# Weighted sum of values in an attention stage: values stationary on four column groups of 32, exponentials streamed

## The chip, the cores and the metric

The kernel runs on one core of a Trainium2 chip. The metric is the device time of one execution in microseconds. The profile shows one execution instruction by instruction, on five engines: PE (TensorE, with its weight loads shown apart as PEld), DVE (VectorE), ACT (ScalarE), POOL (GpSimd) and SP (SyncE, which issues DMAs here).

## What is computed

Two layers on an image of 48 channels and 256 x 256 pixels. Layer 0 normalises by groups, makes queries, keys and values by a pointwise product and a 3 x 3 depthwise convolution, cuts them into 4 x 4 patches and runs an attention of 8 heads over the patches. Layer 1 normalises again and multiplies windows of 64 x 64 along width, height and channels. The part that the change touches is the attention:

```python
        qkv = jnp.einsum('bchw,oc->bohw', x, w_qkv)
        qkv = dwconv3x3(qkv, w_dw)
        q, k, v = jnp.split(qkv, 3, axis=1)
        def heads(t):
            u = unfold(t)
            return u.reshape(b, NUM_HEADS, u.shape[1] // NUM_HEADS, u.shape[2])
        q, k, v = (heads(q), heads(k), heads(v))
        q = _l2norm(q)
        k = _l2norm(k)
        attn = jnp.einsum('bhcn,bhcm->bhnm', q, k) * temperature
        attn = jax.nn.softmax(attn, axis=-1)
        out = jnp.einsum('bhcn,bhnm->bhcm', v, attn)
```

A head has 96 channels. Inside the image there are 4,096 patches, which the kernel treats as n (queries) and m (keys); patches of the border are zeros and enter as a constant in the denominators. The softmax runs over m for each n, and the output is a sum over n: for each head, out[c, m] = sum over n of v[c, n] / z[n] * e[n, m], where e are exponentials of logits and z their sums.

## The kernel before

**Heads and iterations.** The attention stage is a loop over 8 heads (`h`), and in each over 16 iterations (`g`) of two blocks of 128 queries. The order of instructions on every engine in this loop is the order in which the program is written (`manual_schedule`)[...].

In one iteration:
- `normalised` (L585 to L591, VectorE, four short instructions) adds the sums of a block's exponentials, takes the reciprocal and scales the block's values into `vn`, 128 queries by 96 channels.
- `scores` (L337 on TensorE and L572 on ScalarE) makes the logits of one block against all 4,096 keys, in four pieces of 1,024, and their exponentials `e`. It is called for the second block of this iteration and then for the first block of the next, so that ScalarE's work lies under TensorE's.
- `weigh` (L601) makes the weighted sums of the iteration's two blocks, in four parts `k` of 8 key blocks. The stationary operand is 64 columns of `e` (64 keys), the streamed operand is `vn` (96 columns): the result has keys on the partitions, 64 at a time, in two column groups of the array. Each part is 32 matmuls; the trace shows each of them, being fp32, as two instructions. Each part fills one tile of the pool `big` (three tiles of two PSUM banks, which the logits and the strips use too).
- VectorE adds each part to an accumulator in SBUF (`oacc`, L612, 128 x 768; L610, a copy, in a head's first iteration).

**Stores.** The result has keys on the partitions, but memory wants channels there. In a head's last iteration, `store` transposes the accumulators on TensorE (L618, four transposes for 512 keys, into a tile of the pool `one`), copies them with ScalarE (L621) and stores them with two DMAs issued by GpSimd (L623). Parts of the last iteration's sums are stored while the next part is computed; the last two pieces of 512 keys follow in the next head's iteration 0, after its logits, or after the loop for the last head.

**The pool `one`** has two PSUM banks, given out in turn. In it lie `pn` (L247, the norms of a row of depthwise work, read by VectorE at L251), `pst` (L555, the next head's values turned by TensorE, copied by ScalarE at L557; two tiles in each of g = 11 to 14, and one in each of g = 1 to 6 of head 0) and `pt` (above).

**Work of the next head in the same loop.** Heads 0 to 6 carry the depthwise convolution of the following head, ten rows of patches, one row started in each iteration from g = 0 on. In iteration g, VectorE does the norm (about twelve short instructions, L251 to L268) and the scale (L274) of row g-2, and eight taps (L228) of row g-1: three after the scale, five after the second `normalised`. All this comes in VectorE's queue ahead of the iteration's adds. ScalarE squares row g-1 (L239) after the taps; VectorE sums the squares (L243) after the first add. TensorE's `pn` of row g-1 comes at the start of the next iteration. Head 0 also has strips (L177 and L180), TensorE and ScalarE work that the second and fourth parts of `weigh` are followed by.

Of the kernel before, what the change touches and what calls it, by code (L numbers as in the profile page):

```python
# [8 lines left out]
F32 = mybir.dt.float32  # L9
# [13 lines left out]
NH = 8  # L23
HD = C * KK // NH
# [15 lines left out]
TP = 256  # L40
# [5 lines left out]
def conv_preact_kernel(  # L46
# [15 lines left out]
    nc = tc.nc  # L62
# [15 lines left out]
    os_ = dram.tile([NT // TP, C * KK, TP], F32, name="os_")  # L78
# [3 lines left out]
    ident = const.tile([128, 128], F32, name="ident")  # L82
# [15 lines left out]
    for s in range(2):  # L98
        r = slice(s * C, (s + 1) * C)
        for h in range(NH if s == 0 else H0):  # L100
            o = s * M0 + h * HC if h < H0 else (h - H0) * HC
            nc.gpsimd.dma_start(
                out=(wq[r] if h < H0 else wr[0:C])[:, o : o + HC].rearrange("c (z e) -> c z e", z=3),
                in_=w_qkvT.rearrange("c (z h e) -> h c z e", z=3, h=NH)[h],
# [4 lines left out]
    for z in range(3):  # L109
        for j in range(CH):  # L110
            p = (z * CH + j) * 6
# [50 lines left out]
    class Strip:  # L162
# [24 lines left out]
        def store(self):  # L187
            for s, rows in enumerate(both_halves(t1[1], 2 * self.j, 2, base=1)):
                nc.sync.dma_start(out=rows, in_=self.ot[:, 2 * s : 2 * s + 2, :])
# [111 lines left out]
    NB = NT // 128  # L301
    G = 2
    NM = NT // 512
# [99 lines left out]
    with tc.tile_pool(name="xn", bufs=1) as xnp, tc.tile_pool(name="cst", bufs=1) as cst, tc.tile_pool(  # L403
        name="nps", bufs=2, space=PSUM
# [9 lines left out]
        for i, LR in enumerate(parts):  # L414
            j = sum(parts[:i])
# [12 lines left out]
        for g, (w, k) in enumerate(((wq, P2), (wr, C))):  # L428
            m = w.shape[1]
# [98 lines left out]
    with tc.tile_pool(name="ahead", bufs=2) as ah, tc.tile_pool(name="ae", bufs=3) as ae, tc.tile_pool(  # L528
        name="asm", bufs=6
    ) as asm, tc.tile_pool(name="ao", bufs=1) as ao, tc.tile_pool(name="big", bufs=3, space=PSUM) as big:  # L530
        MB = 8
        NK = NB // MB
        NLATE = 1
        RP = TP // PX * KS
        NG = NB // G
        keys, queries, values, oaccs = {}, {}, {}, {}
# [54 lines left out]
            nc.vector.tensor_scalar_mul(vn, values[h, nb // 4][:, nb % 4, :], rz)  # L591
            return e, vn

        def weigh(h, g, blocks, k):

            ps = big.tile([128, 2, 512], F32, name="big")
            for j in range(MB):
                mb = k * MB + j
                for i, (e, vn) in enumerate(blocks):
                    for p in (0, 64):  # L600
                        nc.tensor.matmul(  # L601
                            ps[p : p + 64, j // 4, j % 4 * HD : (j % 4 + 1) * HD],
                            lhsT=e[:, mb * 128 + p : mb * 128 + p + 64],
                            rhs=vn,
                            start=(i == 0),
                            stop=(i == G - 1),
                        )
            if g == 0:
                oaccs[h, k] = ao.tile([128, 2, 4 * HD], F32, name="oacc", bufs=5)
                nc.vector.tensor_copy(oaccs[h, k], ps[:, :, : 4 * HD])  # L610
            else:
                nc.vector.tensor_add(oaccs[h, k], ps[:, :, : 4 * HD], oaccs[h, k])  # L612

        def store(h, m):

            pt = one.tile([HD, 4, 128], F32, name="pt", tag="one")
            for i in range(4):
                nc.tensor.transpose(pt[:, i, :], oaccs[h, m // 2][:, m % 2, i * HD : (i + 1) * HD], ident)  # L618
            late = h == NH - 1 and m >= NM - NLATE
            oo = (pe if late else asm).tile([HD, 512], F32, name="oo", bufs=NLATE if late else 2)  # L620
            nc.scalar.copy(oo, pt.rearrange("p i n -> p (i n)"))  # L621
            for i in range(512 // TP):
                nc.gpsimd.dma_start(  # L623
                    out=os_[m * (512 // TP) + i, h * HD : (h + 1) * HD, :], in_=oo[:, i * TP : (i + 1) * TP]
                )

        load_query(0, 0)
# [14 lines left out]
        with tc.manual_schedule():  # L642
            load_query(0, 1)
            block = scores(0, 0)
            for h in range(NH):
                more = h + 1 < NH
                rows = {r: Depthwise(h + 1, r) for r in range(CR + 1)} if more else {}
                for g in range(NG):
                    p, d, n = rows.get(g - 2), rows.get(g - 1), rows.get(g)

                    if not more and g == 0:
                        convolution.close()
                        early = ExitStack()
                        pe = early.enter_context(tc.tile_pool(name="pe", bufs=1, side="right"))
                        xts = [pe.tile([P2, RP, W], F32, name=f"xt{t}") for t in range(NX)]
                    if h == 0 and 0 < g <= 6:
                        load_value(0, g + 1)
                    if more and CR + 2 <= g < CR + 6:
                        for m in range(2):
                            load_value(h + 1, (g - CR - 2) * 2 + m)  # L660
                    if more and CR + 3 <= g < CR + 6:
                        for m in range(2):
                            load_key(h + 1, (g - CR - 3) * 2 + m)

                    blocks = [normalised(*block)]
                    if p:
                        p.norm()
                        p.root()
                    block = scores(h, g * G + 1)
                    if more and g == NG - 1:  # L670
                        load_key(h + 1, 6)
                        load_key(h + 1, 7, nc.gpsimd)
                    if g + 2 < NG:
                        load_query(h, g + 2)
                    elif more:
                        load_query(h + 1, g + 2 - NG)
                    if p:
                        p.scale()
                    if d:
                        for t in range(1, 4):  # L680
                            d.tap(t)
                    second = block
                    if g + 1 < NG:
                        block = scores(h, (g + 1) * G)
                    elif more:
                        block = scores(h + 1, 0)
                    blocks.append(normalised(*second))
                    if d:
                        for t in range(4, 9):
                            d.tap(t)  # L690

                    if g == 0 and rows:
                        rows[0].load()

                    if h == 0 and 0 < g <= 6:
                        turn(0, g + 1)
                    if more and CR + 2 <= g < CR + 6:
                        for m in range(2):
                            turn(h + 1, (g - CR - 2) * 2 + m)
                    if g == 0 and h > 0:  # L700
                        for m in range(6, 8):
                            store(h - 1, m)
                    if p:
                        p.patches()
                        p.store((2,))
                        p.high()
                    if d:
                        d.square()
                    if n:
                        n.first()  # L710
                    for k in range(NK):
                        s = (h * NG + g) * NK + k
                        weigh(h, g, blocks, k)
                        if k == 0 and d:
                            d.reduce()
                        if k == 0 and p:
                            p.low(nc.gpsimd)
                            p.store((0, 1))
                        if s % 2:
                            for w in strips[s - 1] + strips[s]:  # L720
                                w.run(big.tile([128, 2, 512], F32, name="big"))
                            for w in strips[s + 1] + strips[s + 2]:
                                w.load()
                        elif s:
                            for w in strips[s - 2] + strips[s - 1]:
                                w.store()
                        if k == 2 and g + 1 in rows:
                            rows[g + 1].load()
                        if not more and 0 < g <= 2 * NX and k in (1, 3):
                            i = (g - 1) * 2 + k // 2  # L730
                            t, y = i // 4, i % 4 * (RP // 4)
                            for half in range(2):
                                y0 = half * HALF + t * RP + y
                                nc.sync.dma_start(
                                    out=xts[t][half * C : (half + 1) * C, y : y + RP // 4, :],
                                    in_=xc[:, y0 : y0 + RP // 4, :],
                                )

                        if g == NG - 1 and k > 0:
                            for m in range(2 * k - 2, 2 * k):  # L740
                                store(h, m)
            for m in range(6, 8):
                store(NH - 1, m)
    attention.close()


# [249 lines left out]
```

## Time and profile before

| what | value |
|---|---|
| median of 3 runs | 3673.2 us (3668.67 to 3677.88) |
| span of the profiled execution | 3669.5 us |
| attention stage in it | about 272 to 3227 us |
| mean granted clock of TensorE | 0.976 |
| DVE oacc L612 | 480 of 954 ns |
| PE pt L618 (transposes for the stores) | 256 instructions, 34.4 us busy |
| ACT oo L621 copies, 96 x 512 | 0.58 us each |
| POOL L623 DMA issues | 128 of about 0.51 us |

The page's busy figures are shares of the whole span. Each engine's instructions can be seen in order in the timeline, with the start, the duration, and, in brackets, the idle time before it and what ended it. TensorE's records overlap each other, since its matmuls are pipelined, so the distance between starts says more than a duration does.

### The profile page before, as it was taken

How to read it: one execution, taken by the hardware profiler on the slowest of the kernel's cores; microseconds unless marked ns; L12 is line 12 of the kernel's file. 1: busy time of each engine (PE TensorE's matmuls, PEld its weight loads, DVE VectorE, ACT ScalarE, POOL GpSimd, SP SyncE). 2: the span in 40 equal slices, each digit the busy share in tenths (PEclk: the TensorE clock that was granted, in tenths of full speed). 3: DMA queues.
4: the chain of work that ended last, by engine and by line, in shares of the span. 5: the costliest groups of instructions: out<-in, count | busy, mean ns of one | idle time of the engine just before them, and what ended most of it. 6: DMA issues, size and time to landing. Idle time of an engine off the chain costs nothing.

```text
span 3669.5 us, 100344 instructions
## 1 busy us (share of the span) xinstructions
PE 3466.2 (94%) x44252; PEld 2907.3 (79%) x44252; DVE 2139.8 (58%) x3518; ACT 1873.5 (51%) x2747; POOL 542.7 (15%) x630
## 2 busy tenths in 40 slices
PE   2869999999999999999999999999999999965998
PEld 1337788889988888889899988888899888833776
DVE  5464674179628952895389439934993222267654
ACT  0235676566646654665466556655664444400332
POOL 2030211012211211121112112211221100010011
PEclk9989999999999999999999999999999999976999
DMA  7455665533322332333233323332333220089674
GB/s 161 154 131 147 180 171 168 158 97 92 94 72 82 98 90 80 83 93 87 78 82 92 94 76 87 86 93 71 94 84 87 65 53 19 15 213 240 116 136 93
DMA packets 275427, 386.49 MB, mean 105 GB/s; under 512 B 77330, under 2 KB 211842, under 8 KB 270952
## 3 DMA queue, kind: packets, MB, share of 16 engines
q1 hardware_dynamic: 235942, 264.95, 27.3%
q0 software_dynamic: 35552, 106.40, 12.6%
q10 hardware_dynamic: 3490, 8.64, 1.1%
q8 instruction: 350, 5.73, 0.7%
q14 instruction: 93, 0.76, 0.1%
HBM read 234.76 MB, written 144.90 MB: 103 GB/s over the span
## 4 chain that ended last, share of the span: by engine, by line
PE 84%; DVE 3%; issue 2%; DMA 2%; ACT 1%; SPq 0%; POOL 0%; ACTq 0%; POOLq 0%; DVEq 0%
PE big L337 37%; PE big L601 36%; PE pb L896 4%; PE pa L874 2%; PE pc L913 2%; DVE acc L228 1%; PE big L177 1%; PE pt L618 1%; PE pn L247 1%; DMA pot<-os__70 1%; PE pst L555 1%; DMA x1s<-pxt 0%; DMA kt<-qkv 0%; DMA t<-ot 0%; DVE ss L243 0%
## 5 line engine op out<-in xcount | busy, mean ns | idle before, releaser
L572 ACT ACTIVATE e<-big,nmx 128x1024 f32<-128x1024 f32 x1024 | 1143.9, 1117 | 878.4 <-PE big L337 617.5
L337 PE MATMUL big<-kt,qt 128*128 128x512 f32 x6144 | 1437.5, 393 | 30.2 <-DMA kt<-qkv 29.3
L601 PEld LDWEIGHTS big<-vn,e 128*64 128x64 f32 x32768 | 1358.6, 137 | 57.8 <-ACT e L572 30.6
L601 PE MATMUL big<-vn,e 128*64 128x96 f32 x32768 | 1388.9, 247 | 6.5 <-DVE oacc L612 3.0
L337 PEld LDWEIGHTS big<-kt,qt 128*128 128x128 f32 x6144 | 1146.3, 188 | 277.3 <-issue 29.2
L612 DVE TENSOR_TENSOR oacc<-big,oacc 128x768 f32<-128x768 f32 x480 | 453.5, 954 | 713.4 <-PE big L601 713.4
L228 DVE SCALAR_TENSOR_TENSOR acc<-pad,dwt,acc 126x1024 f32<-126x1024 f32 x592 | 765.6, 1293 | 39.5 <-ACT acc L209 23.7
L295 POOL DMA_DIRECT2D qkv<-o x72 | 52.7, 732 | 1242.2 <-ACT o L279 1242.2
L585 DVE TENSOR_REDUCE zt<-zs 128x1 f32<-128x4 f32 x256 | 38.5, 150 | 335.7 <-ACT e L572 335.7
L289 POOL TENSOR_TENSOR ol<-o,oh 126x1024 fp32r<-126x1024 f32 x78 | 184.6, 2367 | 311.6 <-DVE ss L243 238.9
L572 ACT ACTIVATION_READ_ACCUMULATOR e<-big,nmx 128x1 f32 x1024 | 196.4, 192 | 0.0
L903 ACT COPY lyt<-pb 128x512 f32<-128x512 f32 x144 | 84.3, 586 | 201.6 <-PE pb L896 201.6
L881 DVE TENSOR_TENSOR lzt<-pa,cbias 128x864 f32<-128x864 f32 (+1 forms) x88 | 137.0, 1628 | 85.3 <-PE pa L874 85.3
L279 ACT COPY o<-acc 126x1024 f32<-126x1024 f32 x74 | 158.6, 2143 | 0.0
L896 PEld LDWEIGHTS pb<-wsb,lzt 128*64 128x64 f32 x2304 | 125.9, 138 | 29.4 <-issue 19.7
L896 PE MATMUL pb<-wsb,lzt 128*64 128x128 f32 x2304 | 141.9, 279 | 2.8 <-issue 1.6
L623 POOL DMA_DIRECT2D os__70<-oo x128 | 64.9, 513 | 534.4 <-ACT oo L621 533.8
L790 PE MATMUL pps<-pot,wp 96*96 96x512 f32 x128 | 78.0, 777 | 55.2 <-DMA pot<-os__70 44.3
L239 ACT ACTIVATE sq<-acc 126x1024 f32<-126x1024 f32 x74 | 78.2, 1057 | 101.6 <-DVE acc L228 101.6
L180 ACT ACTIVATE ot<-big,bias 108x1024 f32<-108x1024 f32 x64 | 68.2, 1110 | 111.1 <-PE big L177 62.8
L209 ACT ACTIVATE acc<-pad,dwt 126x1024 f32<-126x1024 f32 x74 | 84.1, 1137 | 79.9 <-DMA pad<-t 79.9
L243 DVE TENSOR_REDUCE ss<-sq 126x64 f32<-126x1024 f32 x80 | 97.5, 1219 | 24.6 <-ACT sq L239 24.6
(127 smaller groups left out, 1904.8 us busy)
## 6 DMA issues: line engine op xcount, KB each, us to landing
pad<-t SPq DMA_DIRECT2D x238, 254.0 KB
t<-ot SPq DMA_DIRECT2D x128, 217.7 KB
qkv<-ol POOLq DMA_DIRECT2D x78, 336.0 KB, 6.4
qkv<-oh POOLq DMA_DIRECT2D x70, 336.0 KB, 5.6
qt<-qkv SPq DMA_DIRECT2D x176, 96.0 KB
xs<-in_x_dram SPq DMA_DIRECT2D x128, 96.0 KB
os__70<-oo POOLq DMA_DIRECT2D x128, 96.0 KB, 2.1
pot<-os__70 SPq DMA_DIRECT2D x16, 768.0 KB
```

The source lines that it names most:

```text
L209: nc.scalar.mul(self.acc, self.pad[:, 0:KS, 0:W], dwt[:, self.h, 0:1])
L228: nc.vector.scalar_tensor_tensor(self.acc, self.pad[:, dy : dy + KS, dx : dx + W], dwt[:, self.h, tap : tap + 1], self.acc, ALU.mult, ALU.add,
L243: nc.vector.tensor_reduce(self.ss, self.sq.rearrange("p a (x b) -> p x a b", b=KS), AX.XY, ALU.add)
L279: nc.scalar.copy(self.o.rearrange("p (a b) x -> p a b x", a=KS), self.acc.rearrange("p a (x b) -> p a b x", b=KS))
L289: eng.tensor_sub(self.ol, self.o, self.oh.bitcast(F32))
L337: nc.tensor.matmul(ps[:, i, :], lhsT=qt[:, r, q0 : q0 + 128], rhs=kts[2 * j + i][:, r // 2, :], start=(r == 0), stop=(r == 2),)
L572: nc.scalar.activation(e[:, j * 1024 : (j + 1) * 1024], ps.rearrange("p a b -> p (a b)"), AF.Exp, bias=nmx[:, b : b + 1], accum_out=zs[:, ...
L601: nc.tensor.matmul(ps[p : p + 64, j // 4, j % 4 * HD : (j % 4 + 1) * HD], lhsT=e[:, mb * 128 + p : mb * 128 + p + 64], rhs=vn, start=(i == 0),
L612: nc.vector.tensor_add(oaccs[h, k], ps[:, :, : 4 * HD], oaccs[h, k])
L881: nc.vector.tensor_tensor(zv[:, :, y0 : y0 + n, :], pa[:, :, : n * T3 * C].rearrange("p s (y k) -> p s y k", y=n), cbias.rearrange("p (u v ...
L896: nc.tensor.matmul(pb[s * WS : (s + 1) * WS, i, :], lhsT=zts[u][:, t * C + c + i, :], rhs=wsb[:, t, :], start=True, stop=True,)
L903: nc.scalar.copy(yt[:, t, :], pb.rearrange("p i x -> p (i x)"))
```

## The change

`weigh` makes its product the other way round. The stationary operand is now 32 channels of `vn`, the streamed operand 512 columns of `e`, and the result has channels on the partitions, so that it can be stored as it is.

A slot is one PSUM bank of 128 partitions: 96 of them are the head's channels for one piece `m` of 512 keys, in three column groups of 32, and the fourth column group takes 32 channels (`j`) of a piece `last` that three slots share. Six slots cover the 8 pieces: slots 0 to 2 the pieces 0, 1, 2 and together 3; slots 3 to 5 the pieces 4, 5, 6 and together 7. A slot is 8 matmuls of 512 columns (four column groups, two blocks).

The four parts of `weigh` become slots (0, 1), (2), (3, 4), (5), and what lay between the parts stays between them. The sums' tile comes from the pool `one` and no longer from `big`; VectorE adds 128 x 512, six times. `store` has no transposes and no copy: two DMAs for each slot, issued by GpSimd right after the slot's last add is issued, take the accumulator to memory, 96 partitions to one piece and 32 to the shared one. The accumulators have eight buffers of 512 instead of five of 768.

```diff
-        MB = 8
-        NK = NB // MB
-        NLATE = 1
+        NK = 4
+        NS = 3
+        SLOTS = [(0, 1), (2,), (3, 4), (5,)]
...
-        def weigh(h, g, blocks, k):
-
-            ps = big.tile([128, 2, 512], F32, name="big")
-            for j in range(MB):
-                mb = k * MB + j
-                for i, (e, vn) in enumerate(blocks):
-                    for p in (0, 64):
-                        nc.tensor.matmul(
-                            ps[p : p + 64, j // 4, j % 4 * HD : (j % 4 + 1) * HD],
-                            lhsT=e[:, mb * 128 + p : mb * 128 + p + 64],
-                            rhs=vn,
-                            start=(i == 0),
-                            stop=(i == G - 1),
-                        )
+        def parts_of(slot):
+
+            q, j = divmod(slot, NS)
+            return q * (NS + 1) + j, q * (NS + 1) + NS, j
+
+        def weigh(h, g, blocks, slot):
+
+            m, last, j = parts_of(slot)
+            ps = one.tile([128, 512], F32, name="pv", tag="one")
+            for i, (e, vn) in enumerate(blocks):
+                for p in range(NS + 1):
+                    c, n = (p, m) if p < NS else (j, last)
+                    nc.tensor.matmul(
+                        ps[p * 32 : (p + 1) * 32, :],
+                        lhsT=vn[:, c * 32 : (c + 1) * 32],
+                        rhs=e[:, n * 512 : (n + 1) * 512],
+                        start=(i == 0),
+                        stop=(i == G - 1),
+                    )
             if g == 0:
-                oaccs[h, k] = ao.tile([128, 2, 4 * HD], F32, name="oacc", bufs=5)
-                nc.vector.tensor_copy(oaccs[h, k], ps[:, :, : 4 * HD])
+                oaccs[h, slot] = ao.tile([128, 512], F32, name="oacc", bufs=8)
+                nc.vector.tensor_copy(oaccs[h, slot], ps)
             else:
-                nc.vector.tensor_add(oaccs[h, k], ps[:, :, : 4 * HD], oaccs[h, k])
-
-        def store(h, m):
-
-            pt = one.tile([HD, 4, 128], F32, name="pt", tag="one")
-            for i in range(4):
-                nc.tensor.transpose(pt[:, i, :], oaccs[h, m // 2][:, m % 2, i * HD : (i + 1) * HD], ident)
-            late = h == NH - 1 and m >= NM - NLATE
-            oo = (pe if late else asm).tile([HD, 512], F32, name="oo", bufs=NLATE if late else 2)
-            nc.scalar.copy(oo, pt.rearrange("p i n -> p (i n)"))
-            for i in range(512 // TP):
+                nc.vector.tensor_add(oaccs[h, slot], ps, oaccs[h, slot])
+
+        def store(h, slot):
+
+            m, last, j = parts_of(slot)
+            T = 512 // TP
+            for p0, p1, n, c in ((0, HD, m, 0), (HD, 128, last, j * 32)):
+                rows = os_[n * T : (n + 1) * T, h * HD + c : h * HD + c + p1 - p0, :]
                 nc.gpsimd.dma_start(
-                    out=os_[m * (512 // TP) + i, h * HD : (h + 1) * HD, :], in_=oo[:, i * TP : (i + 1) * TP]
+                    out=rows.rearrange("t c n -> c t n"),
+                    in_=oaccs[h, slot][p0:p1].rearrange("c (t n) -> c t n", t=T),
                 )
...
-                    if g == 0 and h > 0:
-                        for m in range(6, 8):
-                            store(h - 1, m)
...
-                        weigh(h, g, blocks, k)
+                        for slot in SLOTS[k]:
+                            weigh(h, g, blocks, slot)
+                            if g == NG - 1:
+                                store(h, slot)
...
-                        if g == NG - 1 and k > 0:
-                            for m in range(2 * k - 2, 2 * k):
-                                store(h, m)
-            for m in range(6, 8):
-                store(NH - 1, m)
```

## The prediction

> **What bounds the kernel now.** I read the page's busy shares, then its chain of waits, then single iterations of the attention stage in the timeline.
>
> ```profile
> PE 3466.2 (94%) x44252; PEld 2907.3 (79%) x44252; DVE 2139.8 (58%) x3518; ACT 1873.5 (51%) x2747; POOL 542.7 (15%) x630
> ...
> PE 84%; DVE 3%; issue 2%; DMA 2%; ACT 1%; SPq 0%; POOL 0%; ACTq 0%; POOLq 0%; DVEq 0%
> PE big L337 37%; PE big L601 36%; PE pb L896 4%; PE pa L874 2%; PE pc L913 2%; DVE acc L228 1%; PE big L177 1%; PE pt L618 1%; PE pn L247 1%; DMA pot<-os__70 1%; PE pst L555 1%; DMA x1s<-pxt 0%; DMA kt<-qkv 0%; DMA t<-ot 0%; DVE ss L243 0%
> ```
> TensorE is the path; 37% of the span is logits (L337), 36% the weighted sum (L601) that is changed. One iteration that carries depthwise work (head 3, timeline of TensorE):
> ```profile
> 1987.46 10.78 PE L601 MATMUL big<-vn,e 128*64 128x96 f32 x256
> 1998.18 0.43 PE L247 MATMUL pn<-ss,same 126*126 126x64 f32 x2
> 1998.42 11.15 PE L337 MATMUL big<-kt,qt 128*128 128x512 f32 x48
> 2009.50 10.78 PE L601 MATMUL big<-vn,e 128*64 128x96 f32 x256
> 2020.21 0.43 PE L247 MATMUL pn<-ss,same 126*126 126x64 f32 x2
> ```
> There is no gap: the period is 2020.21 - 1998.18 = 22.03 us. VectorE in the same iteration (timeline of VectorE):
> ```profile
> 1998.29 0.96 DVE L612 TENSOR_TENSOR oacc<-big,oacc 128x768 f32<-128x768 f32 x1 [0.72 <-PE big L601]
> ...
> 2004.39 3.92 DVE L228 SCALAR_TENSOR_TENSOR acc<-pad,dwt,acc 126x1024 f32<-126x1024 f32 x3
> ...
> 2009.00 6.56 DVE L228 SCALAR_TENSOR_TENSOR acc<-pad,dwt,acc 126x1024 f32<-126x1024 f32 x5
> 2015.47 0.95 DVE L612 TENSOR_TENSOR oacc<-big,oacc 128x768 f32<-128x768 f32 x1
> 2016.68 1.22 DVE L243 TENSOR_REDUCE ss<-sq 126x64 f32<-126x1024 f32 x1 [0.26 <-ACT sq L239]
> ```
> The reader should see that VectorE works without a pause from the last add of one iteration (1998.29) to the first add of the next (2015.47), through norm, scale and taps. The first block of sums was complete about 2009.50 + 2.8, yet its add starts 5.97 us after the block's first matmul, 3 us late. Before, nobody minds: a block takes 64 matmuls (2.64 us), and three big buffers let TensorE run on to block 3, 7.9 us in.
>
> **What the Trainium skill says.** "TensorE: Matmul & The Clock Gate", Part 3 (packing small matmuls), says that column groups of 32 run concurrently, but measured 2.38 times for three, not 3. The trace has two column groups (L601) and, in L913, two row by two column groups, never four column groups. "VectorE: DVE Perf Modes", the section on the TRN2 errata, prices a fp32 tensor_tensor at (N+151)/0.96 ns; for 768 that is 957, and the trace has 954. The TensorE page's section on HAM oscillation says that idle gaps above some 3 us halve TensorE's clock; the trace shows it already after less, see below. "TensorEngine Tiling (Array Packing)", PSUM Bottleneck, warns that evacuation may bind after tiling; here it does not by throughput, but by its place in VectorE's queue.
>
> **The change part by part.**
>
> *Matmul time.* Before, each of 128 fp32 matmuls is two instructions; the 256 run in pairs, one in each column group, whose starts lie 82.5 ns apart in the trace: 128 x 0.0825 = 10.56 us, and with the last one's drain the 10.72 from 1987.46 to 1998.18. After, it is 48 matmuls, 96 instructions of 512 columns. L913, 512 columns in four array tiles, shows weight loads in fours:
> ```profile
> 3482.06 0.15 PEld L913 LDWEIGHTS pc<-lyt,hsb 64*64 64x64 f32 x4 [0.28 <-issue]
> 3482.49 0.15 PEld L913 LDWEIGHTS pc<-lyt,hsb 64*64 64x64 f32 x4 [0.28 <-issue]
> ```
> so four go in 0.43 us. If four column groups do the same, an iteration takes 24 x 0.4295 = 10.31 us, a slot 1.718. Gain 0.25 us per iteration. Bounds: nothing lost (10.31) to two streams only (20.6). I take 10.31: the multiply work is equal, and weight loads are fewer (half the columns in 96 instead of 256 instructions) and hidden.
>
> *The adds.* Six of 512 at (512+151)/0.96 = 0.69 us (skill, above; the trace has none) = 4.14 instead of 4 x 0.954 = 3.82 us. VectorE has 22.03 us to do it in where it is not late; nothing on the path by itself.
>
> *The new wait.* Sums move from the big pool (3 buffers) to "one" (2 buffers of a bank), shared with pn and pst. In an iteration the ring goes pn, slot 0, 1, ... 5. The order of instructions shows slot 2 and each later slot waiting for VectorE: slot 2 needs add 0 done. Behind it on TensorE stands everything. From pn's start P: before, add 3 ends at P+1.07, the next iteration's first add comes at P+17.29 (16.22 of chain). After, the last add starts where slot 5 has drained: slot 5's start + 1.718 is P, and an add starts 0.1 us after the last matmul record ends (0.589 long, from L913), so P+0.28; it ends P+0.97; the chain gives add 0 at P+17.19, done P+17.88, TensorE goes on at P+17.94. Slots 2 to 5 take 6.87: period 24.81 instead of 22.03, +2.78 us. The stall: weigh starts at P+11.31, slot 2 could go at P+14.75, so 3.2 us idle. The reduce and adds 1 to 4 then finish before they are needed (add 2 some 1 us ahead).
>
> *The clock.* The last iteration of before has a short idle time; windows cut at the clock's own steps:
> ```profile
> 3206.86:3210.27 3.41, 1.54 (x26) 1.02 (x26) 0.75 (x4) 1.49 (x4) 0.00 (x0) 1.00 0.00 0
> 3210.27:3213.68 3.41, 3.41 (x48) 3.41 (x46) 0.00 (x0) 0.00 (x0) 0.00 (x0) 0.50 0.11 21
> ```
> Columns: length, busy of PE, PEld, DVE, ACT, POOL, clock, DMA. 1.54 busy of 3.41 us was followed by one stretch at half clock. The 1.63 us gap at 315.4 us was not. A stall of 3.2 us leaves at least 1.5 idle in some stretch, mostly more. Half clock in the next 3.41 us costs 1.7 us, less when part of it falls into the stall: on average 1.4, and I count nine in ten: 1.35 us. Slots 2 to 5 are on the path then, so all of it counts. Bounds: 0 to 1.7.
>
> Iterations with both a row in norm and one in taps are g = 2 to 10; in heads 1 to 6 the timeline has the first add at 5.8 to 6.0 us in each: 54 x (2.78 + 1.35) = +223 us. In head 0 strips (L177) give VectorE time: first add 4.2 us in (g to 6) or 4.54 (after). Adding 0.69 + 0.06 against 3.44 gives 1.5 x 5 + 1.86 x 4 = +15. At g = 1, 3.16: 6 x 0.48 = +3.
>
> *Turns.* Values of the next head are turned at g = 11 to 14 of heads 0 to 6, two each:
> ```profile
> 1001.99 0.82 PE L555 MATMUL pst<-ident,vt 96*128 96x96 f32 x8
> 1002.74 3.44 PE L601 MATMUL big<-vn,e 128*64 128x96 f32 x78
> ...
> 1003.29 0.85 ACT L557 COPY vT<-pst 128x384 f32<-128x384 f32 x2
> ```
> (the first two from TensorE's timeline, the third from ScalarE's). Both "one" buffers hold pst, and ScalarE copies them only after its last exponential; the first copy ends at 1003.76, while slot 0 would start at 1002.74. New wait 1.08 x 28 = +30 us. It is 1.1 us, too short for the clock.
>
> *Faster matmuls* where no stall already counts them: 128 - 54 = 74 iterations x 0.25 = -18.5 us.
>
> *Stores.* The transposes (L618) and copies (L621) go. g = 15 takes 24.97 and g = 0 of the next head 22.68 against 21.81 for a bare iteration: 4.03 x 7 = 28; head 7 has two on the path inside (2 us); after its last matmul (3224.04) the first load of the next stage issued at 3232.24, and an add (1.1) and two issues (L623 took 0.51 for 96 rows of 1 KB; now 192 and 64 rows, 1.4 estimated) and their landing (2.1) leave some 5 less, between 2 and 7. Together -35. POOL issues 96 DMAs instead of 128 for the same bytes and rows, at g = 15, behind the last key loads, where POOL is idle. At 1.4 us a slot it keeps pace with 1.72. ScalarE's 64 copies were not on the path. The wait of a new head's first copies for these DMAs is covered by 11 us of logits and by eight oacc buffers.
>
> Sum: +223 + 15 + 3 + 30 - 18.5 - 35 = +217.5. The profiled execution's span is 3669.5, so 3887; the median of the runs is 3673.2, 3.7 above that span, so **3891 us**.
>
> **The rivals.**
> 1. *The stall without the clock's drop* (the stretches count as busy enough). 54 x 1.35 = 73 less: 3818. For it: only one such event lies in the attention stage. Against: its idle share was smaller than what comes.
> 2. *Four column groups do not stream at once* (four fp32 operands read together, or hi and lo passes in order). Two at a time: 128 x 10.3 = +1318; the stall at slot 2 then goes (slots of 3.44 reach 6.87, add 0 is done at 6.6), turns stay: 3673 + 1318 + 30 - 35 = 4986. For it: the skill's 2.38 for three; against: L913's four at once.
> 3. *Faster*: VectorE is not late. If norm, scale and taps ended 3.2 us earlier relative to slot 0, so that add 0 is done within 3.44 us of weigh's start, only gains and turns stay: 3673 - 32 - 35 + 30 = 3636. It decides at that 3.44. The page's VectorE share, 58%, speaks for it; the unbroken row of 17 us against it, since nothing of it is removed.
>
> **How the numbers follow.** The forecast with stall and clock has 0.62 (3840 to 3945 by itself, from 0.9 to 1.7 us of clock loss, and 4% on the slots), rival 1 0.17, rival 2 0.12, rival 3 0.07, and 0.02 for stalls so small that they cancel the gains. What is told from no change is 0.3%, 11 us. Range 3790 to 3960: forecast and rival 1. Faster 0.07, same 0.02, slower 0.91.
>
> **What would show it.** Right: TensorE idle about 3 us before slot 2 of the weighted sum, released by VectorE's add, in g = 2 to 10 of heads 1 to 6; clock below 1 there; periods of 25 to 26.5 us; 21.6 in head 7; four 512-column matmuls each 0.43 us; a 1.1 us wait for ScalarE's copy at g = 11 to 14. Wrong: such matmuls at 0.86, or slot 2 starting 3.44 us in.

## The result and the profile after

The changed kernel takes 3848.3 us (median of four, 3844.57 to 3850.84) against 3674.1 (3668.67 to 3677.88) before: a ratio of 1.0474, 95% interval 1.0458 to 1.049. It is slower, by 174 us; the forecast was 3891, and the range 3790 to 3960 holds the time. The profiled execution's span is 3849.0 us, 179.5 more than before, and the mean granted clock fell from 0.976 to 0.966.

First the page of the changed kernel: busy shares, and the two groups of instructions that the change is about (line, engine, operation, result and operands, shapes, count; then busy time and mean ns of one; then the idle time just before them and what ended it).

```profile
PE 3459.6 (90%) x23516; PEld 1907.3 (50%) x23516; DVE 2176.5 (57%) x3774; ACT 1842.9 (48%) x2683; POOL 534.3 (14%) x598
...
L606 PE MATMUL pv<-e,vn 128*32 128x512 f32 x12288 | 1408.2, 610 | 181.0 <-DVE oacc L617 151.7
...
L617 DVE TENSOR_TENSOR oacc<-pv,oacc 128x512 f32<-128x512 f32 x720 | 491.2, 690 | 876.5 <-PE pv L606 876.5
```

TensorE has half the instructions (23516 instead of 44252) and is busy for practically as long, 3459.6 us instead of 3466.2, but its share fell from 94% to 90%. Before its weighted sums it now stands idle for 181 us (6.5 in the kernel before), 151.7 of them ended by VectorE's add of an earlier slot. An add takes 690 ns.

Where the idle time lies is read from TensorE's timeline. Two iterations of head 2 in a row (start and duration in us; in brackets the idle time before, and what ended it):

```profile
812.72 0.43 PE L247 MATMUL pn<-ss,same 126*126 126x64 f32 x2
812.96 11.18 PE L337 MATMUL big<-kt,qt 128*128 128x512 f32 x48
824.07 3.64 PE L606 MATMUL pv<-e,vn 128*32 128x512 f32 x32
830.36 7.07 PE L606 MATMUL pv<-e,vn 128*32 128x512 f32 x64 [2.65 <-DVE oacc L617]
837.36 0.43 PE L247 MATMUL pn<-ss,same 126*126 126x64 f32 x2
...
848.67 3.64 PE L606 MATMUL pv<-e,vn 128*32 128x512 f32 x32
855.00 8.77 PE L606 MATMUL pv<-e,vn 128*32 128x512 f32 x64 [2.68 <-DVE oacc L617]
863.70 0.43 PE L247 MATMUL pn<-ss,same 126*126 126x64 f32 x2
```

Slots 0 and 1 (32 instructions) run at once, then TensorE stands until an add is done. Starts say more than the bracket: slot 2 follows slot 1's last group by 830.36 - 824.07 - 7 x 0.43 = 3.28 us where 0.43 would do. The first iteration takes 837.36 - 812.72 = 24.64 us, the second 863.70 - 837.36 = 26.34. The difference is in the last 64 instructions, 7.07 and 8.77 us for the same work. VectorE in the first of the two:

```profile
823.14 6.56 DVE L228 SCALAR_TENSOR_TENSOR acc<-pad,dwt,acc 126x1024 f32<-126x1024 f32 x5
829.62 1.28 DVE L617 TENSOR_TENSOR oacc<-pv,oacc 128x512 f32<-128x512 f32 x2
830.83 1.22 DVE L243 TENSOR_REDUCE ss<-sq 126x64 f32<-126x1024 f32 x1
832.35 0.69 DVE L617 TENSOR_TENSOR oacc<-pv,oacc 128x512 f32<-128x512 f32 x1 [0.30 <-PE pv L606]
```

Slot 0 takes four groups of 0.43 us, so it was complete about 1.9 us after 824.07 (with the last group's drain); its add starts at 829.62, right after five taps, and 0.74 us later slot 2 starts. Later adds wait for TensorE and not the reverse.

The two lengths of an iteration are the clock. Three pairs of neighbouring stretches of the changed kernel, cut at the clock's own steps of 3.41 us (columns: length; busy time and instructions of PE, PEld, DVE, ACT, POOL; clock; DMA share; GB/s):

```profile
1756.77:1760.18 3.41, 1.38 (x16) 0.48 (x20) 3.37 (x5) 2.20 (x3) 0.13 (x1) 1.00 0.29 51
1760.18:1763.59 3.41, 3.41 (x40) 1.02 (x36) 1.69 (x3) 0.10 (x1) 3.02 (x2) 1.00 0.02 5
...
2842.21:2845.62 3.41, 1.35 (x16) 0.45 (x20) 3.38 (x5) 2.22 (x3) 0.53 (x1) 1.00 0.37 68
2845.62:2849.03 3.41, 3.41 (x24) 0.87 (x20) 1.03 (x2) 0.13 (x1) 2.99 (x2) 0.50 0.39 147
...
852.23:855.65 3.42, 0.74 (x12) 0.29 (x12) 3.38 (x5) 2.21 (x3) 0.73 (x1) 1.00 0.27 50
855.65:859.06 3.41, 3.41 (x20) 0.87 (x16) 1.73 (x2) 0.82 (x1) 2.29 (x1) 0.50 0.42 125
```

A stretch with 1.38 us busy (2.03 idle) is followed by full clock, 40 instructions; one with 1.35 busy (2.06 idle) by half clock, 24 instructions. All 54 iterations g = 2 to 10 of heads 1 to 6 (the deep iterations, in the words of the expectations below) have the same stall, 2.64 to 2.69 us in the bracket, but the grid of stretches cuts it in different places: 28 take 24.64 us, 25 take 26.34 and one 26.05.

Last the turns, g = 11 to 14 (the first two lines from TensorE's timeline of the changed kernel):

```profile
1027.88 0.83 PE L555 MATMUL pst<-ident,vt 96*128 96x96 f32 x8
1029.71 6.64 PE L606 MATMUL pv<-e,vn 128*32 128x512 f32 x60 [1.00 <-ACT vT L557]
```

and from ScalarE's:

```profile
1029.09 0.19 ACT L572 ACTIVATION_READ_ACCUMULATOR e<-big,nmx 128x1 f32 x1
1029.19 0.85 ACT L557 COPY vT<-pst 128x384 f32<-128x384 f32 x2
```

Slot 0 waits for the first copy of `pst`, which starts after the last exponential: the first sum starts 2.06 us after the start of the last score instruction, instead of 0.99.

The difference in span, from the start of each iteration's scores in both traces:

| where | after less before, us |
|---|---|
| g = 2 to 10 of heads 1 to 6, 54 iterations: 54 x 2.61 + 25 x 1.69 + 1.41 | +184.6 |
| g = 2 to 10 of head 0 | +17.3 |
| g = 11 to 14 of heads 0 to 6, 28 iterations | +23.5 |
| g = 1 of heads 1 to 6 | +0.9 |
| g = 15 and g = 0 of all heads, the rest of head 7, g = 1 of head 0 | -45.5 |
| before the first scores, and after the last sums | +3.7, -5 |
| sum, and between the spans | +179.5 |

The +3.7 is scatter: kernels below, whose code ahead of this stage is the same, begin its scores between 270.9 and 278.4 us.

### The profile page after: what moved, and what is told of

The parts are those of the page before. It is cut to its first block, busy times and chain, and to the rows that moved or that the text cites. A ratio compares the mean times of both kernels' runs of the same rounds, so it can differ in the third digit from the quotient of the medians.

```text
span 3849.0 us, 58896 instructions
## 1 busy us (share of the span) xinstructions
PE 3459.6 (90%) x23516; PEld 1907.3 (50%) x23516; DVE 2176.5 (57%) x3774; ACT 1842.9 (48%) x2683; POOL 534.3 (14%) x598
## 3 DMA queue, kind: packets, MB, share of 16 engines
q1 hardware_dynamic: 235942, 264.95, 26.4%
## 5 line engine op out<-in xcount | busy, mean ns | idle before, releaser
L606 PE MATMUL pv<-e,vn 128*32 128x512 f32 x12288 | 1408.2, 610 | 181.0 <-DVE oacc L617 151.7
L617 DVE TENSOR_TENSOR oacc<-pv,oacc 128x512 f32<-128x512 f32 x720 | 491.2, 690 | 876.5 <-PE pv L606 876.5
L606 PEld LDWEIGHTS pv<-e,vn 128*32 128x32 f32 x12288 | 386.8, 112 | 1123.1 <-issue 748.1
L289 POOL TENSOR_TENSOR ol<-o,oh 126x1024 fp32r<-126x1024 f32 x78 | 184.6, 2367 | 292.0 <-DVE ss L243 218.6
L625 POOL DMA_DIRECT2D os__70<-oacc x96 | 56.3, 591 | 424.8 <-DVE oacc L617 421.0
L217 PE MATMUL dps<-pad,diag 126*126 126x512 f32 x216 | 96.4, 606 | 15.4 <-DMA pad<-t 15.4
```

The lines of the kernel that those rows point to most:

```text
L217: nc.tensor.matmul(ps[:, i, :], lhsT=diag[:, tap, :], rhs=self.pad[:, y : y + 2, dx : dx + W], start=(tap == 0), stop=(tap == 8),)
L289: eng.tensor_sub(self.ol, self.o, self.oh.bitcast(F32))
L606: nc.tensor.matmul(ps[p * 32 : (p + 1) * 32, :], lhsT=vn[:, c * 32 : (c + 1) * 32], rhs=e[:, n * 512 : (n + 1) * 512], start=(i == 0), sto ...
L617: nc.vector.tensor_add(oaccs[h, slot], ps, oaccs[h, slot])
```

## The experiments

The theory was that the loss has two causes, both from the ring of two one-bank tiles: slot 2 waits for an add that stands behind taps, and turns hold both tiles; the clock adds to the first. The rival was that the new form of matmul itself costs something (rate or weight loads). Before was measured beside each group of kernels, at 3676.2 and 3676.5 us.

**The ring taken away everywhere.** Two slots share a tile of two banks from `big`, and both adds come after the second slot.

```diff
-            ps = one.tile([128, 512], F32, name="pv", tag="one")
+            if slot % 2 == 0:
+                pair[0] = big.tile([128, 2, 512], F32, name="big")
+            ps = pair[0][:, slot % 2, :]
...
+            if slot % 2 == 0:
+                return
+            for q in (slot - 1, slot):
...
-                nc.vector.tensor_add(oaccs[h, slot], ps, oaccs[h, slot])
+                    nc.vector.tensor_add(oaccs[h, q], pair[0][:, q % 2, :], oaccs[h, q])
...
```

> The changed kernel with the sums of two slots in one two-bank tile of the pool big (three tiles) instead of one-bank tiles of the pool with two; both adds come after the second slot. Theory (the ring of two banks makes slot 2 wait for a late add, and slot 0 wait for the turned values' copy): both waits go, deep iterations fall from 24.6 or 26.3 us to about 21.8, turn iterations from 23.3 to about 22.2, and the whole to 3674 - 32 (matmuls) - 35 (stores) = 3607 us, faster than the kernel before. TensorE's clock is 1 throughout the attention stage. Rival (VectorE is the bound, its work of some 21.5 us an iteration being what counts): deep iterations stay above 24, time stays above 3800. Rival (four column groups are slower than two): above 3700.

Measured: 3610.0 us (3603.08 to 3614.88), 0.9824 of before (0.9807 to 0.984). It is 238 us faster than the changed kernel, and faster than before. One iteration in TensorE's timeline of this kernel:

```profile
807.23 0.43 PE L247 MATMUL pn<-ss,same 126*126 126x64 f32 x2
807.48 11.15 PE L337 MATMUL big<-kt,qt 128*128 128x512 f32 x48
818.56 10.51 PE L609 MATMUL big<-e,vn 128*32 128x512 f32 x96
828.99 0.43 PE L247 MATMUL pn<-ss,same 126*126 126x64 f32 x2
```

All 96 instructions run through: 21.76 us an iteration against 22.03 before. VectorE's queue is as late as ever, the first add coming 6.2 to 6.8 us after the sums begin, and nobody waits for it, since three tiles of two banks let TensorE run ahead. So the matmuls are a gain, and the whole loss goes when the short ring goes. The expectation that the clock stays at 1 was not quite met: in head 0, from 429.5 us on, two stretches ran at half clock.

**The ring taken away at the turns alone.** The same edit, with the tile from `big` only where this holds:

```diff
+            two = h + 1 < NH and CR + 2 <= g < CR + 6
```

> The changed kernel with the sums in the pool big (as e1) only in the 28 iterations that turn values (g = 11 to 14 of heads 0 to 6). Theory (slot 0 waits 1.06 us for the copy of the first turned tile): the gap ahead of the first sum falls from 2.06 to 0.99 us there, 28 x 1.06 = 30 less: 3818 us. Rival (the gap is the array's change of mode or the transposes themselves): no change, 3848.

Measured: 3821.9 us (3820.67 to 3823.7), 1.0394 (1.0377 to 1.0412): 26.4 less than the changed kernel in medians, and 27.1 in the profiled spans. By iterations, those of the turns in heads 1 to 6 are 1.08 us shorter each, where 1.06 was expected, and the deep ones on average the same to 0.01 us. The turns' price is shown to be separate.

**The clock by itself.** Seven matmuls into a tile that nobody reads fill part of the stall, in g = 2 to 10 of heads 1 to 6. They add work and take no wait away; what the kernel computes is unchanged.

```diff
+                            if slot == 2 and p and d and h > 0:
+                                fill = big.tile([128, 2, 512], F32, name="big")
+                                for i in range(7):
+                                    nc.tensor.matmul(
+                                        fill[:, i % 2, :],
+                                        lhsT=queries[h, g + 1][:, 0, 0:128],
+                                        rhs=keys[h, 0][:, 0, :],
+                                        start=True,
+                                        stop=True,
+                                    )
```

> The changed kernel with seven extra 512-column matmuls (1.55 us at full clock, into a tile that nobody reads) ahead of slot 2 in the 54 deep iterations of heads 1 to 6, where TensorE stands still for 3.25 us. Theory (26 of these 54 are followed by a stretch at half clock, which costs 1.69 each): no stretch is idle enough any more, all 54 take 24.64 us, 3848 - 44 = 3804 us, with more work on TensorE. Rival (the second kind of iteration, 26.33 us, has another cause, such as VectorE or ScalarE late): no change, 3848, or longer.

Measured: 3802.4 us (3799.61 to 3806.13), 1.034 (1.0323 to 1.0357). In TensorE's timeline of this kernel:

```profile
832.38 0.43 PE L247 MATMUL pn<-ss,same 126*126 126x64 f32 x2
...
843.72 3.64 PE L606 MATMUL pv<-e,vn 128*32 128x512 f32 x32
847.29 1.88 PE L717 MATMUL big<-kt,qt 128*128 128x512 f32 x7
850.02 7.08 PE L606 MATMUL pv<-e,vn 128*32 128x512 f32 x64 [0.84 <-DVE oacc L617]
857.02 0.43 PE L247 MATMUL pn<-ss,same 126*126 126x64 f32 x2
```

Slot 2 starts as late as in the changed kernel, 6.30 us after the sums begin (6.29 there), and every one of the 54 iterations now takes 24.64 us, none at half clock: 43.9 us less in these iterations. TensorE does more and the kernel is 46 us faster. The split of the loss, 141 for the stall and 44 for the clock, is shown by this run.

**The late engine moved instead.** If the add is late because of taps, three taps put behind adds 0, 1 and 2 should do as well as a deeper ring. The first form moved the square and the sum of squares along, and nothing else:

```diff
-                        for t in range(4, 9):
+                        for t in range(4, 6 if p else 9):
...
-                    if d:
+                    if d and not p:
...
+                            if p and d and slot < 3:
+                                d.tap(6 + slot)
+                            if p and d and slot == 2:
+                                d.square()
+                            if p and d and slot == 3:
+                                d.reduce()
```

> The changed kernel with its two-bank ring, but where a row is in norm and one in taps, taps 6, 7 and 8 come behind adds 0, 1 and 2 in VectorE's queue (the square behind them, the sum of squares behind add 3). Nothing is removed. Theory (add 0 is late by its place behind the taps): add 0 starts about 2.0 to 2.3 us after the first matmul instead of 5.57, slot 2 does not wait, deep iterations take about 21.8 to 22.0 us, head 0 loses its stalls too, turns keep theirs: 3640 us (3630 to 3665). Rival (VectorE's amount of work binds): deep iterations still at 24 or more, above 3800.

Measured: 4316.9 us (4315.83 to 4319.48), 1.1744 (1.1725 to 1.1764). A miss by 677 us. ScalarE's timeline of this kernel:

```profile
828.58 1.15 ACT L209 ACTIVATE acc<-pad,dwt 126x1024 f32<-126x1024 f32 x1
841.97 1.06 ACT L239 ACTIVATE sq<-acc 126x1024 f32<-126x1024 f32 x1 [12.24 <-DMA qkv<-ol]
```

and TensorE's:

```profile
824.21 8.79 PE L606 MATMUL pv<-e,vn 128*32 128x512 f32 x80
833.86 1.92 PE L606 MATMUL pv<-e,vn 128*32 128x512 f32 x16 [0.86 <-DVE oacc L617]
844.94 0.68 PE L247 MATMUL pn<-ss,same 126*126 126x64 f32 x2 [9.15 <-DVE oacc L617]
```

The stall at slot 2 is gone: slots 0 to 4, 80 instructions, run through. But the square stands idle for 12.24 us, until the store of `ol` has landed. `sq` and `ol` (the low part of a row's result, made by GpSimd) share one buffer, and moving the square put it after `ol` in the program instead of ahead of it. The sum of squares, the last adds and `pn` follow, TensorE stands for 6 to 11 us, and with the half clock after that (the mean is 0.915) iterations take 30 to 37 us. The second form moves GpSimd's low part and its stores behind the sum of squares too, so that the buffer's order is the old one:

```diff
                             if p and d and slot == 3:
                                 d.reduce()
+                                p.low(nc.gpsimd)
+                                p.store((0, 1))
...
-                        if k == 0 and p:
+                        if k == 0 and p and not d:
```

> As e2_taps, but the low part of row g-2 (POOL, L289) comes behind the sum of squares in the program, so that the square does not have to wait until the low part's buffer, which it shares, has been stored; in e2_taps that wait took up to 14 us. Theory (the place of the taps makes add 0 late, and the late add makes the stall): add 0 starts about 2 us after the first matmul, deep iterations take 21.8 to 22.1 us with TensorE's clock at 1, head 0 loses its stalls, turns keep theirs: 3640 us (3630 to 3665), faster than the kernel before with a ring of two banks. Rival (the ring of two is too short for VectorE's amount of work whatever the order): deep iterations above 23.5, 3780 or more.

Measured: 3663.9 us (median of seven, 3656.77 to 3665.14), 0.9962 (0.995 to 0.9974). TensorE's timeline of this kernel:

```profile
812.33 10.73 PE L606 MATMUL pv<-e,vn 128*32 128x512 f32 x96
823.47 0.43 PE L247 MATMUL pn<-ss,same 126*126 126x64 f32 x2 [0.41 <-DVE oacc L617]
823.71 11.15 PE L337 MATMUL big<-kt,qt 128*128 128x512 f32 x48
```

No stall inside the sums, clock 0.977, and the kernel is slightly faster than before with the ring of two banks still there. It misses the expected 3640 by 24 us: adds 4 and 5 now follow the late sum of squares, so `pn` waits 0.41 us, and an iteration takes 22.5 us instead of the 21.8 that g = 2 alone has.

To give a point between none and three, one tap alone (tap 8, with the square after it) was put behind add 1; the sum of squares, the low part and its stores follow slot 2.

```diff
-                        for t in range(4, 9):
+                        for t in range(4, 8 if p else 9):
...
+                            if p and d and slot == 1:
+                                d.tap(8)
+                                d.square()
+                            if p and d and slot == 2:
+                                d.reduce()
+                                p.low(nc.gpsimd)
+                                p.store((0, 1))
...
```

> The changed kernel with only tap 8 moved behind add 1 (square, sum of squares and low part follow it). Theory: add 0 starts one tap, 1.30 us, earlier (4.27 instead of 5.57), deep iterations take 23.34 instead of 24.64, and as the stall is then 1.95 us, none of them leaves a stretch of 3.41 us idle for 2.03 us or more, so none is followed by half clock: 3848 - 70 (54 x 1.30) - 44 (26 x 1.69) - 12 (head 0) = 3722 us. Rival (the clock falls after any stall of this kind, or at half a stretch): some iterations of 25.0, 3745 or more. Rival (the stall isn't set by add 0): 3848.

Measured: 3717.4 us (3714.26 to 3718.46), 1.0107 (1.0087 to 1.0127). In TensorE's timeline:

```profile
822.56 3.64 PE L606 MATMUL pv<-e,vn 128*32 128x512 f32 x32
827.55 7.07 PE L606 MATMUL pv<-e,vn 128*32 128x512 f32 x64 [1.35 <-DVE oacc L617]
```

The bracket is 1.35 instead of 2.65, one tap of 1.28 us less; iterations take 23.3 us, and none of them is at half clock. One tap is worth 131 us of the median. By iterations of the profiled executions: 54 x 1.32 = 71 of stall in heads 1 to 6, 44 of clock, and 22 in head 0; parts outside these iterations take some 5 back.

**The order of the column groups.** Does the rate need the four groups in turn? The tiles are those of the first experiment, and in a slot the loops are swapped, so that each column group's two blocks (four instructions) follow each other in the program.

```diff
-            for i, (e, vn) in enumerate(blocks):
-                for p in range(NS + 1):
-                    c, n = (p, m) if p < NS else (j, last)
+            for p in range(NS + 1):
+                c, n = (p, m) if p < NS else (j, last)
+                for i, (e, vn) in enumerate(blocks):
```

> e1_big with the two loops of the weighted sum exchanged: the two blocks of one column group follow each other, so that four instructions in a row (two matmuls of two passes) go to the same group. Theory (TensorE starts only what comes next in the program, and the four groups run together because the program names them in turn): groups overlap only at the seams, a slot takes up to 5.6 us instead of 1.72, and the time goes up by as much as 2970 us, to some 6600. Rival (each column group takes its own instructions, whatever stands between): no change, 3610.

Measured, one run: 3630.3 us. The theory of a strict order falls. On this kernel's page the group reads

```profile
L609 PE MATMUL big<-e,vn 128*32 128x512 f32 x12288 | 1368.0, 594 | 3.4 <-ACT ot L180 2.1
```

1368.0 us busy against 1348.6 in the first experiment. In the trace four instructions start within some 40 to 90 ns, then four more 0.43 us later, a slot still takes 1.72 us, and the deep iterations 21.83 to 22.07 instead of 21.76. The records don't name the column group, so what follows is inferred from the order of the program and these times: a column group takes its own work while instructions of another group stand ahead of it. The order costs some 20 us, by one run (13 of them in the deep iterations), and not a factor.

**One add for two slots.** The first experiment with a single add of 128 x 1024 for each tile of two banks.

```diff
...
-                nc.vector.tensor_add(oaccs[h, slot], ps, oaccs[h, slot])
+                nc.vector.tensor_add(oaccs[h, slot // 2], pair[0], oaccs[h, slot // 2])
...
```

> e1_big with one add of 128 x 1024 for two slots instead of two of 128 x 512. Theory (with the stalls gone TensorE is the bound, VectorE is not): VectorE works some 0.15 us less in each pair and nothing else changes: 3605 to 3612 us, the same as e1_big. Rival (VectorE binds in deep iterations of e1_big): up to 54 x 0.45 = 24 us less, 3586.

Measured: 3605.4 us (3603.19 to 3614.12), 0.9813 (0.979 to 0.9835). The page of this kernel has

```profile
L623 DVE TENSOR_TENSOR oacc<-big,oacc 128x1024 f32<-128x1024 f32 x360 | 440.0, 1222 | 692.6 <-PE big L609 692.6
```

An add of 1222 ns stands for two of 685, 23 us less of busy time in these adds, and the time is that of the first experiment within the spread of both; a deep iteration takes 21.76 us in either. The adds' amount of work bounds nothing here. This is the lowest median of all, though not told apart from 3610.0; either beats both kernels.

## Why the prediction was right, and what it mis-sized

The direction, the place and the mechanism were right; the total was 43 us too high. Of these, 38 are in the sum below, 29 in one term of it. The other 5 are the step from span to median: the profiled execution of before lay 4 us under its median, that of after 1 us over.

| term of the prediction | predicted, us | measured, us |
|---|---|---|
| wait at slot 2, 54 iterations | 54 x 2.78 = 150 | 54 x 2.61 = 141 |
| clock in these iterations | 54 x 1.35 = 73 | 25 x 1.69 + 1.41 = 44 |
| head 0, g = 2 to 10, with its faster matmuls | 15 - 2 = 13 | 17.3 |
| g = 1 of heads 1 to 6, with their faster matmuls | 3 - 1.5 = 1.5 | 0.9 |
| turns, with their faster matmuls | 30 - 7 = 23 | 23.5 |
| stores, the other 31 iterations' matmuls, start and tail | -35 - 8 = -43 | -46.8 |
| sum (before rounding) | 217.5 | 179.5 |

- *Matmul time.* Right. Four of 512 columns start every 0.43 us, 7 ns apart from each other; an iteration without a wait takes 21.54 us instead of 21.81, 0.27 less (0.25 predicted). The second rival, four groups not streaming at once, 4986 us, fell with that. The first experiment says the same by its time.
- *The wait at slot 2.* Right to 0.17 us an iteration. Add 0 starts 829.62 - 812.72 = 16.90 us after `pn`, where 17.19 was predicted: the last add comes 837.50 - 837.36 = 0.14 after the next `pn` and not 0.28, and the chain from there is 0.15 shorter. Slots 2 to 5 took 7.00 us and not 6.87, which gives 0.13 of that back.
- *The clock.* This term was mis-sized, 44 us for 73: "A stall of 3.2 us leaves at least 1.5 idle in some stretch, mostly more. [...] and I count nine in ten". The mechanism held, but the stall was shorter by the records, 2.65 us, and the bound higher. The stretches are a fixed grid of 3.41 us, and in these iterations those with up to 2.03 us idle were followed by full clock, those with 2.06 or more by half. A stall of 2.65 us, laid at random on such a grid, leaves more than 2.05 us in one stretch in (0.76 + 2 x 0.6) / 3.41 = 57% of cases; 26 of 54 are 48%. With the bound of 1.5 us it would have been (0.76 + 2 x 1.15) / 3.41 = 90%, and a stall of 3.2 us leaves 1.6 or more in every case; how the prediction came to nine in ten it does not say. The event that it showed had 3.41 - 1.54 = 1.87 us idle, and even that bound would have given 68%. The gap of 1.63 us that it set against this event lay across two stretches, with some 1.2 us in the second, and so said little. The other factor erred to the other side: a half-clock stretch cost the full 1.69 us and not 1.4, since in 25 of the 26 slot 2 had begun before the slow stretch did (in the other 0.54 us after it, and there the loss is 1.41). And 0.9 x 1.4 is 1.26, where 1.35 was carried, which is 5 us of the excess.
- *Head 0.* The sum comes near by luck. A stall of 1.5 us was predicted in each of g = 2 to 6, but in g = 4 to 6 the first add came 2.0 to 2.6 us after the sums began, and nothing waited for it. Instead two iterations, g = 3 and g = 10, lost 5.5 and 4.3 us, with stretches at half clock in them, which the prediction had left out in head 0. Why VectorE was in time there stays open.
- *The first rival*, the stall without the clock (3818), is half true: it describes 28 of the 54 iterations. The third experiment makes it whole; with all the clock's loss in heads 1 to 6 gone it has 3802.
- *The third rival*, VectorE not late (3636), fell for the changed kernel, but its arithmetic is what the pairs in `big` realise: 3636 less the 30 of the turns is 3606, against 3610.0 and 3605.4 measured.
- *Stores.* g = 15 gains 3.42 us in heads 1 to 6 and g = 0 of the next head 1.14; together 4.56, of which 2 x 0.27 is matmul: 4.02 for the stores, 4.03 predicted. The tail is 5 us shorter, as predicted.

The Trainium skill, page "TensorE: Matmul & The Clock Gate", has in its section "A second HAM failure mode: psum-queue depth-cycling" the closest description of what the change ran into: cycling through PSUM banks each iteration lets TensorE stand idle for short times often enough that the clock goes up and down. The prediction did not use it; it took a gap of "some 3 us" from the section before, which has 3.4. The trace agrees for 26 of the 54 stalls, though the stall itself cost more (141 us) than the clock (44), and it adds a size: here 2.06 us idle of one 3.41 us stretch is enough, where Part 1 of the page speaks of a whole idle window of about 3.4 us.

## What to carry over

When sums move to a ring of accumulator tiles, count how far TensorE can run ahead of the slowest add: two banks were 3.4 us of run-ahead where the first add began 5.6 us after the sums, and with a pool of six banks the same change made the kernel 1.8% faster instead of 4.7% slower. Throughput does not show this; an engine at 57% with a long unbroken row ahead of the add does. And before moving work out of that row, list every buffer that it shares: what frees the add can tie the moved instruction to a transfer.

## What the runs showed of the hardware

- Every step of TensorE's granted clock in these traces lies on a fixed grid of 3.41 us. In the 54 equal stalls of this kernel the next stretch was at half clock when 2.06 us or more of a stretch were idle by the records, some 60%, and at full clock at 2.03 or less. In the kernel with the turns alone in `big`, whose stalls lie elsewhere on the grid, the border is between 2.04 and 2.1. It is no general bound: the event in the kernel before fell at 1.87, and in head 0 half clock followed a stretch with 1.03 us idle in the first experiment's kernel (at 426 us) and one with 0.96 in the kernel with the filling matmuls (at 432). What decides there stays open.
- Work that nobody reads can make a kernel faster: seven matmuls in each stall took 46 us off, 44 of them, by iterations, from the clock.
- Four column groups with fp32 operands run at the full fourfold rate: four instructions of 512 columns start every 0.43 us, where in the kernel before the fp32 instructions of 512 columns in L150, one tile of the array at a time, start mostly 0.42 to 0.43 us apart. They do so even where four instructions of one group follow each other in the program, at some 20 us more in the whole kernel. The Trainium skill's page "TensorE: Matmul & The Clock Gate", Part 3, has matmuls start strictly first in, first out; in this one run a slot's 1.72 us leaves no room for that between different column groups, and the measurement decides.
